# Layer 0 of a two-layer gated attention kernel: scores computed once, weights turned by VectorE and transfers

## The chip, the core and the metric

The kernel runs on one core of a Trainium2 chip. A core has a matrix engine (TensorE, PE in the profile, with its weight loads as PEld), three engines for elementwise work (VectorE or DVE, ScalarE or ACT, GpSimd or POOL), a SyncE (SP) that issues transfers, and 16 DMA engines that carry them out. Each engine works through its own queue in order and waits on semaphores for the others. Matrix products are written to PSUM, a small memory of 128 partitions and eight banks of 512 float32 each; everything else lies in SBUF, also with 128 partitions. The metric is the time of one execution in device microseconds.

## The reference, cut to what matters

Eight batches of 256 tokens of width 256 (`x`) and eight contexts of the same size (`ctx`) pass through two layers, each a gated cross attention followed by a gated feed-forward part. The change touches the first layer's attention:

```python
q, k, v = layernorm(x) @ Wq + bq, ctx @ Wk + bk, ctx @ Wv + bv      # 16 heads of 16
scores  = einsum('bhqd,bhkd->bhqk', q, k) / sqrt(16)
attn    = softmax(scores, axis=-1)                                   # 256 x 256 per head
out     = einsum('bhqk,bhkd->bhqd', attn, v).reshape(...) @ Wo + bo
x       = x + tanh(g_xattn[0]) * out
```

Behind it come a slot-routing feed-forward part per batch ("slots" below), a second attention with 8 heads of 128, where the 256 context rows are the queries' media and 512 keys stand against 256 queries, and a quantized feed-forward part that needs the maximum over all batches.

## The kernel before, in words

**Staging.** A first stretch prepares weights and works on batches 0 and 1 of layer 0 (attention and slots). Then `attention1` runs layer 1's attention, 8 batches x 8 heads, one head a step. Beside it a side queue holds the rest of layer 0, batches 2 to 7 with their slots, cut into pieces with costs. `side.share` works out how much of it is due so that batch b is ready before layer 1 comes to it, and each step spends half of that share after the head's softmax and half at its end. At the last batch the queue is drained, and the weights of the last feed-forward part are prepared. The tile framework schedules the instructions of each engine from this program order and from what it thinks the operations take, so pieces of both layers stand interleaved in every engine's queue. Tiles of a pool rotate through a fixed number of buffers, and a tile's next user waits for its last reader.

**Layer 0's attention for one batch** (`Batch0`). `query` and `key` project 256 tokens at once into one PSUM bank (L554), ACT adds the bias. Scores need more precision than one pass of the fast format float32r gives, so `split` (L520, L522) makes each operand the sum of a high part, rounded to float32r, and a low part; a product over 64 rows (hi hi lo lo against hi lo hi lo) restores it. For batches 0 and 1 `spread` builds these rows with selection matmuls. From batch 2 on, `split` writes the parts to DRAM and `stack` reads them back, with weights whose columns `by_place` has reordered so that a head's elements lie in the right places.

The 16 heads go in four groups of four. For each group the scores are computed twice:

- `scores`: queries on partitions. Eight matmuls of 65 rows (64 and one of blank) put four heads and two halves of the queries into PSUM (L648), VectorE finds each query's maximum (L651, four calls of 128x512), which is again split in two parts (L654, L655).
- `maxima`: one TensorE transposition (L661) and two ACT copies (L664) turn the maxima into rows 64 to 72 of the query operand.
- `exps`: eight matmuls of 73 rows with keys on partitions (L674), in which the maxima are subtracted by the extra rows. ACT takes the exponential of 128x512 at once (L677, four a group). The weights now stand with keys on partitions, as the next product needs them.
- `sums`: sixteen records of products with 32 columns each (L685) give the weighted values and, by a block of ones, the sums; `divide` turns them with a VectorE transposition (L708) and divides.

Layer 0's matmuls from batch 1 on use three PSUM banks, `bank_z`; layer 1 uses four, `bank_m`.

**Layer 1's attention** (`Batch1`) computes its scores once, with queries on partitions (L1170). The maximum (L1171) goes into the exponential as a bias (L1172). Then the weights are turned: VectorE transposes blocks of 32x32 (L1184) into a tile `z` with one buffer, and four transfers from SP (L1190) move the blocks to their partitions (`eT`). The keys are stored in a permuted order for that (`by_block`). `value` fills a tile for a pair of heads in two halves: the context half is copied out by ACT, the other by VectorE (L1147, L1154), both at the odd step before the pair. The query projection is L1087, the key L1124, the sums L1226, the output projection L1239.

The line that takes the scores twice, in `exps`:

```python
T.matmul(ps[:, kc, :], k[:, j, kc * P : (kc + 1) * P], q[:, j, :], start=True, stop=True)
```

Of the kernel before, what the change touches and what calls it, by code (L numbers as in the profile page):

```python
# [21 lines left out]
P = 128  # L22
# [3 lines left out]
HG = 4  # L26
# [23 lines left out]
IDLE_KEY = 10  # L50
IDLE_LATENTS = 8
# [55 lines left out]
def flamingo_kernel(ctx: ExitStack, tc: tile.TileContext, a: dict, out: bass.AP):  # L107
# [62 lines left out]
    wk_n, wq_n = xs[4], cs[4]  # L170
    wk, wq = (w0.tile([P, 2, D], F32, tag=n, name=n) for n in ("wk", "wq"))
    bk_n, bq_n = (pp_.tile([P, 2], F32, tag=n, name=n) for n in ("bkn", "bqn"))
    bk, bq = (w0.tile([P, 2], F32, tag=n, name=n) for n in ("bk", "bq"))
    nc.sync.dma_start(out=cs[0], in_=c_in[0])
    nc.sync.dma_start(out=wk_n, in_=a["L0_xattn_Wk"].rearrange("(c p) n -> p c n", p=P))
    nc.sync.dma_start(out=xs[0], in_=x_in[0])
    nc.sync.dma_start(out=wq_n, in_=a["L0_xattn_Wq"].rearrange("(c p) n -> p c n", p=P))
    for t, name in ((bk_n, "L0_xattn_bk"), (bq_n, "L0_xattn_bq")):
        nc.sync.dma_start(out=t, in_=a[name].rearrange("(c p) -> p c", p=P))
# [14 lines left out]
    def load_by_place():  # L194
        for m in range(2):
            for t, name in ((bk, "L0_xattn_bk"), (bq, "L0_xattn_bq")):
                bias = a[name].rearrange("(h e) -> e h", e=DK0)
                nc.sync.dma_start(out=t[:, m : m + 1], in_=bias[m * 8 : (m + 1) * 8, :])

    def by_place():  # L200
        for t, n in ((wk, wk_n), (wq, wq_n)):
            A.copy(t.rearrange("p c (e h) -> p c e h", e=DK0), n.rearrange("p c (h e) -> p c e h", e=DK0))
        G.tensor_scalar(bq4, bq, DK0**-0.5, None, ALU.mult)

# [4 lines left out]
    pick = w0.tile([NMAX, HG], F32, tag="pick", name="pick")  # L209
    V.tensor_tensor(pick, ident[:NMAX, 1 : 1 + HG], ident[:NMAX, 1 + HG : 1 + 2 * HG], ALU.add)  # L210

    def operand_pairs(pool, n):

        pairs = []
        for i in range(n):
            q = pool.tile([NROW + NMAX, HG, S], F32R, tag=f"qs{i}", name=f"qs{i}")
            k = pool.tile([NROW + NMAX, HG, S], F32R, tag=f"ks{i}", name=f"ks{i}")
            V.tensor_copy(q[NROW : NROW + 1, :, :], blank[:1, :HG, None].to_broadcast([1, HG, S]))
            V.tensor_copy(k[NROW:, :, :], pick[:, :, None].to_broadcast([NMAX, HG, S]))
            pairs.append((q, k))  # L220
        return pairs

    blank = w0.tile([P, 2 * HG], F32, tag="blank", name="blank")
    V.memset(blank, 0.0)

    pairs_a, pairs_b = operand_pairs(pp_, 2), operand_pairs(w0, 2)


# [102 lines left out]
    slotsT = pp_.tile([P, 2, P], F32, tag="slotsT", name="slotsT", bufs=1)  # L331
# [29 lines left out]
    def prepare_slots():  # L361
        st = {}

        def load_slots():
# [7 lines left out]
            st["w2"] = pp_.tile([NSLOT, P], F32, tag="w2n", name="w2n")  # L372
# [92 lines left out]
    bq4_n = pp_.tile([P, 2], F32, tag="bq4n", name="bq4n")  # L465
    G.tensor_scalar(bq4_n, bq_n, DK0**-0.5, None, ALU.mult)

    def values_tile(pool):
# [5 lines left out]
    halved = {  # L474
        s: [pool.tile([P, SIDE + NMAX], F32R, tag=f"nm{s}{i}", name=f"nm{s}{i}") for i in range(3)]
        for s, pool in (("a", pp_), ("b", w0))
    }
    for nm in halved["a"] + halved["b"]:
        V.tensor_copy(nm, blank[:, :1].to_broadcast([P, SIDE + NMAX]))
# [4 lines left out]
    class Batch0:  # L484
# [32 lines left out]
        def split(self, name, full):  # L517
# [7 lines left out]
            name += self.s  # L525
            d = dram.tile([2, D, S], F32, tag=f"d{name}", name=f"d{name}")
            for i, x in enumerate((hi, lo)):
                nc.sync.dma_start(out=d[i].rearrange("(m p) t -> p m t", p=P), in_=x.bitcast(F32))
            return d.rearrange("i (e h) t -> i e h t", e=DK0)
# [9 lines left out]
        def turn_c(self):  # L539
            self.cT = self.pool.tile([P, 2, S], F32, tag="cT", name="cT", bufs=1)  # L540
            A.copy(self.cT, self.turned(cs[self.b]))
# [21 lines left out]
        def query(self):  # L563
            w, bias = (wq_n, bq4_n) if self.b < 2 else (wq, bq4)
# [450 lines left out]
    for n, go in enumerate(first):  # L1015
# [3 lines left out]
        if n >= LAG:  # L1019
            second.pop(0)()  # L1020
# [738 lines left out]
```

## Time and profile before

| | |
|---|---|
| median of 3 runs | 915.75 us (913.85 to 917.1) |
| profiled execution | 917.64 us, span 915.7 us |
| PE busy | 877.0 us (96%) |
| PEld busy | 636.3 us |
| DVE busy | 639.8 us (70%) |
| ACT busy | 461.9 us (50%) |
| POOL busy | 143.1 us |
| bytes moved | 71.12 MB, hardware queue 29.0% of 16 DMA engines |
| granted TensorE clock | 0.992 |

The page gives, for every engine, the time in which at least one instruction ran. A busy PE is not a PE at its peak: matmuls overlap, so the distance from one start to the next is what one costs, and the mean of a group (382 ns for a record of L1226) is longer than that (0.216 us; a float32 matmul has two records). A table of stretches gives the same for parts of the span, named by their ends in microseconds. In the groups, the name before `<-` is the tile written, then come the tiles read, the shapes, the number of instructions, busy time and mean, and after the second bar the idle time of the engine just before them with what ended it. "eT<-z" in the lists of transfers is layer 1's turning of the weights, "qs<-dqb" and "ks<-dkb" are layer 0's stacks.

### The profile page before, as it was taken

How to read it: one execution, taken by the hardware profiler on the slowest of the kernel's cores; microseconds unless marked ns; L12 is line 12 of the kernel's file. 1: busy time of each engine (PE TensorE's matmuls, PEld its weight loads, DVE VectorE, ACT ScalarE, POOL GpSimd, SP SyncE). 2: the span in 40 equal slices, each digit the busy share in tenths (PEclk: the TensorE clock that was granted, in tenths of full speed). 3: DMA queues.
4: the chain of work that ended last, by engine and by line, in shares of the span. 5: the costliest groups of instructions: out<-in, count | busy, mean ns of one | idle time of the engine just before them, and what ended most of it. 6: DMA issues, size and time to landing. Idle time of an engine off the chain costs nothing. (4 is left out here: it accounts for less than half of the span.)

```text
span 915.7 us, 12787 instructions
## 1 busy us (share of the span) xinstructions
PE 877.0 (96%) x4339; PEld 636.3 (69%) x4341; DVE 639.8 (70%) x1630; ACT 461.9 (50%) x915; POOL 143.1 (16%) x183
## 2 busy tenths in 40 slices
PE   5998999999999999999999999999989999999897
PEld 4766777887777767766777667666756776776645
DVE  9675788777587766767677665766895475455387
ACT  3676646555356542555544544554364335434394
POOL 7011130201110112111011000010510010000083
PEclk9999999999999999999999999999999999999999
DMA  6712303342341332332312322212323232222112
GB/s 165 250 10 69 114 29 90 88 120 77 108 116 47 92 92 47 84 98 73 92 37 68 104 69 71 46 47 64 107 64 70 47 69 59 58 55 60 24 35 92
DMA packets 71728, 71.12 MB, mean 78 GB/s; under 512 B 14640, under 2 KB 67184, under 8 KB 71664
## 3 DMA queue, kind: packets, MB, share of 16 engines
q1 hardware_dynamic: 70032, 69.53, 29.0%
q0 software_dynamic: 1632, 0.79, 0.5%
q8 instruction: 35, 0.57, 0.3%
q14 instruction: 29, 0.24, 0.1%
HBM read 28.08 MB, written 8.39 MB: 40 GB/s over the span
## 5 line engine op out<-in xcount | busy, mean ns | idle before, releaser
L1172 ACT ACTIVATE e<-bank_m,nm 128x512 f32<-128x512 f32 x128 | 88.0, 688 | 107.5 <-DVE nm L1171 105.3
L1171 DVE TENSOR_REDUCE nm<-bank_m 128x1 f32<-128x512 f32 x128 | 87.1, 686 | 60.1 <-PE bank_m L1170 59.1
L1226 PE MATMUL bank_m<-eT,v 128*128 128x256 f32 x496 | 121.5, 382 | 4.6 <-DMA eT<-z 4.3
L1226 PEld LDWEIGHTS bank_m<-eT,v 128*128 128x128 f32 x496 | 92.4, 190 | 35.7 <-issue 16.6
L1124 PE MATMUL bank_m<-kvT,w1kv 128*128 128x512 f32 (+1 forms) x256 | 115.9, 568 | 0.0
L1147 PE MATMUL bank_m<-w1kv,kvT 128*128 128x256 f32 x480 | 111.0, 380 | 0.0
L1170 PE MATMUL bank_m<-k,q 128*128 128x512 f32 x224 | 108.9, 598 | 0.0
L1147 PEld LDWEIGHTS bank_m<-w1kv,kvT 128*128 128x128 f32 x480 | 89.4, 190 | 12.0 <-issue 0.8
L1184 DVE STREAM_TRANSPOSE z<-e 128x512 f32<-128x512 f32 x126 | 88.6, 706 | 4.3 <-DMA eT<-z 1.8
L651 DVE TENSOR_REDUCE nf<-bank_z 128x2 f32<-128x512 f32 x112 | 74.0, 680 | 20.7 <-PE bank_z L648 20.6
L270 POOL TENSOR_TENSOR rstd<-rstd,mhalf 128x2 f32<-128x2 f32 x48 | 34.6, 722 | 298.0 <-DVE rstd L269 267.7
L677 ACT ACTIVATE e<-bank_z 128x512 f32<-128x512 f32 x112 | 63.5, 598 | 32.7 <-PE bank_z L674 31.8
L1124 PEld LDWEIGHTS bank_m<-kvT,w1kv 128*128 128x128 f32 x256 | 46.4, 190 | 43.1 <-issue 38.0
L1233 ACT ACTIVATE oT<-bank_m,bv 128x256 f32<-128x256 f32 x64 | 30.4, 474 | 81.1 <-PE bank_m L1226 81.0
L1087 PE MATMUL bank_m<-kvT,w1q 128*128 128x256 f32 x256 | 64.0, 385 | 1.3 <-DVE kvT L1077 0.9
L1174 DVE TENSOR_SCALAR e<-e,rs 128x512 f32<-128x512 f32 x128 | 63.3, 495 | 2.6
L1239 PE MATMUL bank_m<-w1o,oT 128*128 128x256 f32 x256 | 59.2, 380 | 0.6 <-DVE x L1253 0.6
L1170 PEld LDWEIGHTS bank_m<-k,q 128*128 128x128 f32 x224 | 41.0, 191 | 23.4 <-issue 17.0
L1087 PEld LDWEIGHTS bank_m<-kvT,w1q 128*128 128x128 f32 x256 | 48.1, 192 | 12.4 <-issue 3.9
L1239 PEld LDWEIGHTS bank_m<-w1o,oT 128*128 128x128 f32 x256 | 48.0, 190 | 10.2 <-issue 3.2
L674 PE MATMUL bank_z<-qs,ks 73*128 73x256 f32 x224 | 49.8, 325 | 3.2 <-DVE nf L651 2.6
L1154 DVE COPY v<-bank_m 128x512 f32<-128x512 f32 x32 | 22.0, 688 | 44.0 <-PE bank_m L1147 44.0
(386 smaller groups left out, 1482.0 us busy)
## 6 DMA issues: line engine op xcount, KB each, us to landing
eT<-z SPq DMA_DIRECT2D x252, 128.0 KB, 2.7
qs<-dqb SPq DMA_DIRECT2D x96, 64.0 KB, 2.5
ks<-dkb SPq DMA_DIRECT2D x48, 128.0 KB, 2.8
c<-in_ctx_dram SPq DMA_DIRECT2D x8, 256.0 KB, 2.9
x<-in_x_dram SPq DMA_DIRECT2D x8, 256.0 KB, 2.8
w1kv<-in_L_xattn_Wkv_dram SPq DMA_DIRECT2D x4, 512.0 KB, 6.8
out_dram<-y SPq DMA_DIRECT2D x7, 256.0 KB, 2.2
dqb<-hi SPq DMA_DIRECT2D x6, 256.0 KB, 3.0
```

Source lines behind the costliest of these rows:

```text
L651: V.tensor_reduce(full[:, 2 * half : 2 * half + 2], ps, AX.X, ALU.max, negate=True)
L677: A.activation(e[:, i, :, :], ps, AF.Exp)
L1087: T.matmul(pq[:, i, :], w1q[:, c, h * P : (h + 1) * P], self.kvT[:, c, S:], start=c == 0, stop=c == 1,)
L1124: T.matmul(pk[:, at], w1kv[:, c, h * P : (h + 1) * P], self.kvT[:, c, at], start=c == 0, stop=c == 1,)
L1147: T.matmul(pv[:, k, :], (self.mT, self.kvT[:, :, S:])[half][:, c, k * P : (k + 1) * P], w1kv[:, c, at : at + 2 * P], start=c == 0, stop=c ...
L1170: T.matmul(ps, q, self.k[h], start=True, stop=True)
L1171: V.tensor_reduce(nm[:, at], ps, AX.X, ALU.max, negate=True)
L1172: A.activation(e[:, qc, :], ps, AF.Exp, bias=nm[:, at], accum_out=sums[:, at])
L1174: V.tensor_scalar(e[:, qc, :], e[:, qc, :], rs[:, at], None, ALU.mult)
L1184: V.transpose(z[:, :, :, qc, :].rearrange("p kq kc s -> p kc kq s"), self.e[h][:, qc, :].rearrange("p (kc kq k) -> p kc kq k", kc=4, kq=4),)
L1226: T.matmul(pi, self.v[h // 2][kc // 2][:, kc % 2, (h % 2) * P : (h % 2 + 1) * P], eT[:, kc], start=kc == 0, stop=kc == 3,)
L1239: self.projected = T.matmul(self.pp[:, qc, :], self.oT[:, h, qc * P : (qc + 1) * P], w1o[:, h, :], start=h == 0, stop=h == H1 - 1,).ins
```

## The change

From batch 1 on (the attention of batches 1 to 7; what goes through DRAM from batch 2 on), `weigh` replaces `scores`, `maxima` and `exps`. It takes half a group, two heads, in one call:

- A stack now holds two heads in 128 rows, head 0 in rows 0 to 63 and head 1 in 64 to 127 (tile 128x2x256 for a group). Four matmuls of 64 rows, two of each head, fill two banks.
- Per head VectorE finds the maxima (negated), and ACT takes two exponentials of 128x256 with the maxima as bias.
- VectorE transposes 32x32 blocks of 128x512 into `z0` (one buffer), and four transfers from SP bring the blocks to `eT0` (three buffers). `sums` reads `eT0`.
- Keys are stored in a permuted order by the ACT instruction that adds the bias, `turn_o` undoes the order of the queries in two calls.

Around it: the weights are no longer reordered (`by_place`, `load_by_place` and the second weight tiles go). `split` writes sixteen transfers a batch instead of four, `stack` reads two a group instead of six. The piece `weigh` has the cost 1.0, and its two calls for the next group stand before and after `sums` of the current one. Some tiles move into memory that is free early (`cT` of batch 0, the slots' turned states), the tiles of normalised tokens in layer 1 have one buffer instead of two, and layer 1's values have three half tiles instead of two whole ones, with the second half computed after the sums of the even head instead of at the odd step before.

```diff
+        def weigh(self, g, s):
+            q, k = self.pairs[g % 2]
+            ps = [self.bank().rearrange("p (c k) -> p c k", c=2) for _ in range(2)]
+            if s == 0:
+                self.idle(ps[0][:, 0, :], (IDLE_SCORES + ((0,) * NG,) * B)[self.b][g])
+            for qc in range(2):
+                for i in range(2):
+                    at = slice(i * NROW, (i + 1) * NROW)
+                    T.matmul(ps[i][:, qc, :], q[at, s, qc * P : (qc + 1) * P], k[at, s, :], start=True, stop=True)
+            z = at0.tile([P, 8, 2, 2, 32], F32, tag="z0", name="z0", bufs=1)
+            for i in range(2):
+                nm = small.tile([P, 2], F32, tag="nm0", name="nm0")
+                V.tensor_reduce(nm, ps[i], AX.X, ALU.max, negate=True)
+                e = at0.tile([P, 2, S], F32, tag="e", name="e", bufs=2)
+                for qc in range(2):
+                    A.activation(e[:, qc, :], ps[i][:, qc, :], AF.Exp, bias=nm[:, qc : qc + 1])
+                V.transpose(
+                    z[:, :, i, :, :].rearrange("p kb c s -> p c kb s"), e.rearrange("p c (kb k) -> p c kb k", k=32)
+                )
+            eT = self.e[g, s] = at0.tile([P, 4, 2, 2, 64], F32, tag="eT0", name="eT0", bufs=3)
+            for i in range(4):
+                nc.sync.dma_start(
+                    out=eT[:, i].rearrange("p kc h x -> p (kc h x)"),
+                    in_=z[32 * i : 32 * i + 32].rearrange("p kb h c s -> p (kb h c s)"),
+                )
...
@@ split
-            d = dram.tile([2, D, S], F32, tag=f"d{name}", name=f"d{name}")
-            for i, x in enumerate((hi, lo)):
-                nc.sync.dma_start(out=d[i].rearrange("(m p) t -> p m t", p=P), in_=x.bitcast(F32))
-            return d.rearrange("i (e h) t -> i e h t", e=DK0)
+            d = dram.tile([H0 * NROW, S], F32, tag=f"d{name}", name=f"d{name}")
+            for r, x in enumerate((hi, hi, lo, lo) if name == "q" else (hi, lo, hi, lo)):
+                to = d.rearrange("(m h r e) t -> r m h e t", m=2, r=4, e=DK0)[r]
+                for m in range(2):
+                    nc.sync.dma_start(out=to[m], in_=x[:, m, :].bitcast(F32))
+            return d.rearrange("(g s p) t -> g p s t", s=2, p=P)
...
@@ stack
+            for to, d in zip(self.pairs[g % 2], (self.dq, self.dk)):
+                ins = nc.sync.dma_start(out=to.bitcast(F32), in_=d[g])
...
@@ layer0
         def maxima(me, g):
+            if me.b > 0:
+                return [piece(COST_WEIGH, me, "weigh", g, s) for s in range(2)]
...
+                    work, ahead = ahead[:1], ahead[1:]
...
                 work.append(piece(1.8, me, "sums", g))
+                if b > 0:
+                    work += ahead
...
@@ Batch1.value, attention1
+                v = at1.tile([P, 2, 2 * P], F32, tag="v1", name="v1", bufs=3)
...
                 bs[last[0]].sums(last[1])
+            if h % 2 == 0 and n > 0:
+                me.value(h // 2, 1)
...
                     bs[nxt[0]].value(nxt[1] // 2, 0)
-                bs[nxt[0]].value(nxt[1] // 2, 1)
```

## The prediction

> **What bounds the kernel now.** I read the table of stretches first, then the chain of waits in order of time, then the groups by cost and the timeline of TensorE (PE) and SyncE (SP). The stretches were cut by the times of layer 1's score matmuls: its heads 4 to 16 run from 172 to 340 us, heads 16 to 40 from 340 to 641, the last 18 or so without any layer 0 beside them.
>
> ```profile
> core 0: us, PE busy (x) PEld busy (x) DVE busy (x) ACT busy (x) POOL busy (x), PEclk, DMA share, GB/s
> 172.00:340.00 168.00, 164.96 (x868) 123.09 (x867) 121.25 (x330) 86.93 (x176) 21.08 (x26) 0.99 0.34 92
> 340.00:641.00 301.00, 297.61 (x1441) 213.23 (x1440) 209.04 (x551) 145.44 (x293) 32.20 (x43) 1.00 0.27 70
> 700.00:850.00 150.00, 148.74 (x584) 104.56 (x582) 86.93 (x182) 64.64 (x143) 4.57 (x7) 1.00 0.26 59
> ```
>
> PE is busy 98 to 99% in all three, VectorE (DVE) 72, 69 and 58%. From 131 to 650 us layers 0 and 1 share one PE queue, and each microsecond of matmul taken out there should shorten the span, as long as nobody else becomes late.
>
> ```profile
> 143.76 0.83 PE L674 MATMUL bank_z<-qs,ks 73*128 73x256 f32 x4
> 144.42 0.40 PE L648 MATMUL bank_z<-ks,qs 65*128 65x256 f32 x2
> 144.66 0.60 PE L1167 MATMUL bank_m<-c,q 128*128 128x256 f32 x2
> ```
>
> The second scores (L674) hold PE from 143.76 to 144.42, 0.165 us each with the change of kind; two of L648 take 0.24, so 0.12 each. The groups give the rest:
>
> ```profile
> L674 PE MATMUL bank_z<-qs,ks 73*128 73x256 f32 x224 | 49.8, 325 | 3.2 <-DVE nf L651 2.6
> L651 DVE TENSOR_REDUCE nf<-bank_z 128x2 f32<-128x512 f32 x112 | 74.0, 680 | 20.7 <-PE bank_z L648 20.6
> L1184 DVE STREAM_TRANSPOSE z<-e 128x512 f32<-128x512 f32 x126 | 88.6, 706 | 4.3 <-DMA eT<-z 1.8
> L677 ACT ACTIVATE e<-bank_z 128x512 f32<-128x512 f32 x112 | 63.5, 598 | 32.7 <-PE bank_z L674 31.8
> L664 ACT CAST qs<-bank_z 9x512 fp32r<-9x512 f32 x56 | 32.2, 575 | 16.1 <-PE bank_z L661 15.4
> L1233 ACT ACTIVATE oT<-bank_m,bv 128x256 f32<-128x256 f32 x64 | 30.4, 474 | 81.1 <-PE bank_m L1226 81.0
> L654 DVE CAST nmb<-nf 128x4 fp32r<-128x4 f32 x56 | 9.5, 170 | 0.4
> L655 DVE TENSOR_TENSOR nmb<-nf,nmb 128x4 fp32r<-128x4 f32 x56 | 8.8, 156 | 0.5
> eT<-z SPq DMA_DIRECT2D x252, 128.0 KB, 2.7
> 319.65 2.50 SPq L1190 DMA_DIRECT2D eT<-z  x4
> ```
>
> L1184 and the eT transfers are layer 1's own turning of weights, which the change copies into layer 0: 0.706 us of DVE per 128x512, four issues of 2.50 us on SP, 2.7 us to land.
>
> **The change part by part.** A group is four heads of one batch; the new code reaches batches 1 to 7, 28 groups, of which batch 1's four lie before 131 us.
>
> PE. Per group, eight L674 and the transposition of maxima (L661) go; the eight first scores stay. Eight at 0.12 to 0.165 are 0.96 to 1.32 us; L661 takes 0.20 (300.91 to the next start at 301.11). I take 8 x 0.145 + 0.20 = 1.36 us, 38 us in all, 32.6 of it in the shared stretch and 5.4 before.
>
> The first scores change form, from 65 rows to 64 at two row offsets into two banks. If pairs run side by side, they cost half: 56 calls x 0.29 = 16 us less. If they don't, and each call adds a break like that around the 32-column products L685 (16 records in 1.00 us, where 16 x 0.216 / 4 is 0.86), 56 x 0.14 = 8 us more. I take nothing, halfway between unknown ends.
>
> The Trainium skill, "TensorEngine Tiling (Array Packing)", Key Properties, says that changing the tiling mode drains TensorE, which speaks against 64-row calls among full ones; the L685 row shows such a break at 0.14 us at most. The same page promises up to twice the speed at 64 rows or fewer; by the one the sum is 8 us worse, by the other 16 better, and no row here shows which.
>
> DVE. Per group four transpositions of 0.706 come, two L654 and two L655 go: 2.82 - 0.65 = 2.17 us, 61 us over 28 groups. The four maxima keep their size. Turning the output in two halves costs 2 x 0.44 (L708's size) for one of 0.709, 0.2 per batch. Counted in the changed instruction order, 38 maxima fall between heads 4 and 16 and 42 between 16 and 36, 9.5 and 10.5 groups. So in the first stretch DVE has 121 + 21 = 142 us and PE 168 - 13 = 155: 92%. In the second 209 + 23 = 232 against 301 - 14 = 287: 81%. That is the price that has to be found.
>
> How PE fares beside a full DVE the profile shows itself. Of the slices of 25 us from 125 to 675, five have DVE over 20 us: PE is idle there 0.82, 0, 0.28, 0.67 and 0.91 us, on average 0.54, at most 0.91. Over the 440 us that remain that is 9.5 us, at most 16; at least 0, as in the second of them.
>
> ScalarE (ACT). Eight exponentials of 128x256 at 0.474 (L1233's size) replace four of 0.598 and two casts of 0.575: 3.79 for 3.54, 7 us in all on an engine half idle. Nothing; if the cover is gone, 7.
>
> SP and DMA. Per group eight issues of about 0.63 and two stacks replace six (0.79 + 1.81 by the timeline): 5.8 for 2.6 us. Per batch 16 split issues replace four; at 0.38 (L528) to 0.80 (a 32 KB L192 issue) 6 to 13 us for 1.5. Over six batches that is 104 to 146 us more on SP, whose queue then stands at some 60% of the shared stretch instead of a third. 28 MB of weights and 6 MB of split writes join 69.5 MB at 29.0%: 43%. Both stay under their limits, but a 2.5 us burst can now stand ahead of layer 1's own eT, and on SP every transfer waits for its own source with all later ones behind it.
>
> The wait that is new: the weighted sums (L685, now fed by transfers) wait for the landing. From the end of the scores: two maxima 1.4, or one and four exponentials 2.6, one transposition 0.7, three issues 1.9, and 2.7 for the fourth to land: some 7.9 us with every engine free. Layer 1's same chain has a landing of 2.6 to 4.2 alone between 340 and 641 us, so 9 is likelier there. In the changed PE order I summed the matmuls that stand between a group's last scores and its sums: from 7.0 us up, six of 28 under 9. Their shortfalls add to 6.5 us at a latency of 9, to 29 at 11 and to nothing at 7. I take 6.5. Behind the waiting sums on PE stand layer 1's scores, for which DVE and ACT wait.
>
> Moved: layer 1's second half of a value pair (L1147, 1.73 us of PE, one DVE copy of 0.69) goes behind the sums of the next even head, past that head's maxima on DVE and its four eT issues on SP, past nothing on POOL. Its reader is a head later, 8.6 us on PE: nothing; if late, 0.7 per pair. One buffer instead of two for the normalised tokens: its three users stand at separate heads, so nothing; 0.6 (four transpositions) per use if not.
>
> Start. Two sets of setup casts (2 x 0.96 + 2 x 0.81), two 1.05 us ACT copies of weights and four bias loads go. The first key projection starts at 10.90, right after the second context's transpositions at 10.42 that waited for its transfer; the changed order puts two more transpositions and five warm-up matmuls ahead of it, 0 to 1 us later. Of batch 1's 5.4 us I count half, because before 131 us PE is not full (21.8 to 22.9 of 25).
>
> Sum: 32.6 + 2.7 - 9.5 - 6.5 = 19 us off the profiled execution's 917.64 us (span 915.7 and 1.9 around it), that is 898.6. The profiled execution stands 1.9 above the median of 915.75, so I forecast 897.
>
> **Rivals.**
> A, slower: DVE takes the lead through the single z buffer. A second call's transpositions wait until the first's four transfers have read z; DVE works in order, so layer 1's maxima stand behind them and PE runs dry. For: 16 of the calls in the changed PE order follow the one before by under 3 us, while z is held until about 7.9 us after the scores. Against: layer 1's z is single too, and L1184 waits only 1.8 us for it. It decides from 35.3 / 48 = 0.74 us of PE idle per call in the shared stretch, instead of the 0.33 of my sum; at 1.0 it gives 917.6 - 35 + 48, less 1.9: about 929.
> B, faster still: pairs of 64-row scores run side by side and waits stay at the low end: 19 + 16 = 35 less, some of it stopped by DVE's 92%: 878 to 888.
> C, nothing: the sums' latency is 11 us rather than 9. 19 - 22 = -3; with part of it hidden, 912 to 918.
>
> **How the numbers follow.** Mine 0.50, B 0.22, C 0.12, A 0.16. A measurement of this kernel tells about 0.3% (2.7 us) from no change: under 913 is faster, over 918.5 slower. Mine and B are all faster, C splits 0.04, 0.06, 0.02. Faster 0.76, same 0.06, slower 0.18. My own case's range is 887 to 908, from stalls of 7 to 27 us. To leave out two in ten I reach down into B to 877 and up through C to 917; A lies outside.
>
> **What would show it.** Right: no second scores, PE still over 97% in the shared stretch and layer 0's last sums some 30 us earlier; DVE total near 640 + 58 = 698, over 85% busy in the first half of the shared stretch; sums' waits on eT a few us in total. Wrong: PE under 95% with long waits for DVE's maxima or z (A), sums' waits over 20 us (C), or four scores in well under 0.5 us (B).

## The result, and the profile after

The changed kernel takes 944.04 us (median of four runs, 942.1 to 950.09) against 915.06 for the kernel before: a ratio of 1.0326, with a 95% interval of 1.0275 to 1.0376. The forecast was 897, so the step that was to take 19 us away added 29.

The table of stretches of the changed kernel, cut at the same heads of layer 1 (4 to 16, 16 to 40, and the last part without layer 0); the columns are those of the table before:

```profile
core 0: us, PE busy (x) PEld busy (x) DVE busy (x) ACT busy (x) POOL busy (x), PEclk, DMA share, GB/s
186.20:371.90 185.70, 164.72 (x778) 112.97 (x777) 143.97 (x361) 85.26 (x196) 24.98 (x32) 0.94 0.59 157
371.90:670.40 298.50, 289.04 (x1310) 198.01 (x1309) 222.40 (x536) 137.72 (x305) 34.52 (x44) 0.99 0.43 109
735.00:885.00 150.00, 148.73 (x584) 105.62 (x583) 83.32 (x174) 63.31 (x140) 4.57 (x7) 1.00 0.26 59
```

Heads 16 to 40 take 298.5 us instead of 301, and in the last part TensorE is as busy as before. The first row is where time goes: it takes 185.7 us instead of 168, with TensorE busy for the same 165 us: 89% instead of 98. VectorE is at 78% there, not at the 92% forecast, because the stretch is longer. The DMA share went from 0.34 to 0.59, and the granted clock from 0.99 to 0.94. The rest of the loss lies ahead of this table: layer 1's first head starts at 146.8 us instead of 131.2.

The page's totals, the hardware queue's share, and three groups of VectorE:

```profile
PE 868.5 (92%) x4089; PEld 606.0 (64%) x4089; DVE 683.9 (73%) x1631; ACT 447.6 (48%) x961; POOL 141.1 (15%) x182
...
q1 hardware_dynamic: 115952, 105.19, 43.0%
```

```profile
L674 DVE STREAM_TRANSPOSE z<-e 128x512 f32<-128x512 f32 x112 | 75.0, 692 | 30.2 <-DMA eT<-z 26.7
...
L1200 DVE STREAM_TRANSPOSE z<-e 128x512 f32<-128x512 f32 x126 | 87.7, 702 | 3.9 <-DMA eT<-z 2.0
L670 DVE TENSOR_REDUCE nm<-bank_z 128x2 f32<-128x512 f32 x112 | 72.9, 677 | 21.0 <-PE bank_z L666 20.7
```

Of the forecast's quantities the DMA share (43.0%, forecast 43) and a transposition's 692 ns (forecast 706) came out as said. VectorE's total came near (684, forecast 698), though its rise was 44 us and not 58. TensorE's did not: its busy time fell by 8.5 us (877.0 to 868.5) instead of 38, and its idle time, summed over the gaps between matmuls, rose from 30.3 to 64.7. Layer 0's last sums, forecast some 30 us earlier, start 17 us later (604.1 us instead of 587.2).

TensorE's waits in the changed kernel (total, times, longest). Before, its waits for layer 1's eT came to 4.3 (the line shown second), and there were none for a stack (ks, qs, now kt, qt):

```profile
engine line waited for: us in total, times, longest us
PE bank_z L666 <- DMA kt<-dk: 9.4, 4, 3.7
PE bank_m L1242 <- DMA eT<-z: 8.8, 4, 3.6
PE bank_z L693 <- DMA eT<-z: 7.6, 8, 2.0
...
PE bank_z L743 <- DVE oT L736: 4.7, 2, 4.2
```

```profile
PE bank_m L1226 <- DMA eT<-z: 4.3, 3, 2.0
```

**Where TensorE's time went.** Counting each matmul record from its start to the next start (less idle time) gives what a line costs. By that count the second scores (L674 of before) fell by 37.4 us and the transposed maxima (L661) by 5.6: 43.0, where the forecast had 38. The first scores went from 38.1 to 32.7 in batches 1 to 7, the sums of all batches from 33.0 to 35.9. Against that saving of some 46 us, all the other lines together, whose work is unchanged, cost 38 us more, and idle time is 34 us more.

**The clock.** A part of the 38 us is the clock. The clock's record begins 16.3 us into the span of the kernel before and 14.4 us into that of the changed one; the earlier time is left out here, and so is the very end. It has four stretches at half clock in the kernel before, 3.41 us each. In the changed one there are thirteen such units, so nine more: 31 us at half clock, up to 15 us of work lost. They stand behind TensorE's gaps. The stretches around one of them, 3.4 us with a wait for kt, the 6.8 after it, and the next 3.4:

```profile
256.80:260.20 3.40, 0.13 (x1) 0.00 (x0) 0.69 (x1) 0.93 (x3) 0.00 (x0) 1.00 0.85 237
260.20:267.00 6.80, 6.33 (x25) 2.72 (x26) 4.86 (x10) 2.35 (x6) 0.00 (x0) 0.50 0.43 140
267.00:270.40 3.40, 3.40 (x13) 2.05 (x12) 2.70 (x8) 0.79 (x2) 0.00 (x0) 1.00 0.31 93
```

The last column but two is the granted clock: 1.00 while TensorE stood idle, 0.50 for the two units after. In both traces every unit of 3.41 us with 1.8 us or more of idle TensorE is followed by half clock. Those with 1.5 to 1.7 at full clock are not, and some that have 0.7 to 1.4 are. In all nineteen traces of this case, from the start of the clock's record to 12 us before the end, each of the 90 units at full clock with 2.0 us or more of idle is followed by half clock, and 29 of the 90 with 1.5 to 2.0; so the 1.8 of these two traces is no sharp limit. A wait of 2 us within one unit therefore cost 2 here and then up to another 1.7 or 3.4. The Trainium skill ("TensorE: Matmul & The Clock Gate", Part 1) says that the clock halves after an idle window of about 3.4 us; the window's length agrees, but here 2.0 us of idle in a window was enough.

**One of the waits for kt, followed back.** SyncE's queue and TensorE's in the changed kernel (start, duration, line, what is moved):

```profile
start us, us, engine line op out<-in xcount [idle before <-releaser]
324.65 2.48 SPq L679 DMA_DIRECT2D eT<-z  x4
327.24 1.31 SPq L506 DMA_DIRECT2D dk<-hi  x2
328.66 1.19 SPq L506 DMA_DIRECT2D dk<-lo  x2
329.89 1.18 SPq L506 DMA_DIRECT2D dk<-hi  x2
331.12 1.18 SPq L506 DMA_DIRECT2D dk<-lo  x2
332.41 0.57 SPq L604 DMA_DIRECT2D qt<-dq  x1
335.65 0.88 SPq L604 DMA_DIRECT2D kt<-dk  x2
```

```profile
334.39 1.02 PE L1186 MATMUL bank_m<-k,q 128*128 128x512 f32 x2
335.25 0.38 PE L912 MATMUL bank_s<-ident,hn 128*128 128x128 f32 x2
338.47 0.63 PE L666 MATMUL bank_z<-kt,qt 64*128 64x256 f32 x4 [2.84 <-DMA kt<-dk]
```

The next batch's key is split; SP issues its eight writes (L506) from 327.24 to 332.30. The read of kt (L604) needs them landed and goes out at 335.65, and the first scores (L666) start at 338.47, after 2.84 us of nothing on TensorE. Half clock follows from 338.7. Of the four waits for kt in this trace, two are followed at once by half clock, this one and the longest (3.74 us, at 260.67); the other two, 1.25 and 1.57 us, are not. Before, a split had two writes per operand instead of eight.

### The profile page after: what moved, and what is told of

It is laid out like the page before. It is cut to its first block, busy times and chain, and to the rows that moved or that the text cites. A ratio compares the mean times of both kernels' runs of the same rounds, so it can differ in the third digit from the quotient of the medians.

```text
span 941.9 us, 12794 instructions
## 1 busy us (share of the span) xinstructions
PE 868.5 (92%) x4089; PEld 606.0 (64%) x4089; DVE 683.9 (73%) x1631; ACT 447.6 (48%) x961; POOL 141.1 (15%) x182
## 5 line engine op out<-in xcount | busy, mean ns | idle before, releaser
L673 ACT ACTIVATE e<-bank_z,nm 128x256 f32<-128x256 f32 x224 | 90.0, 476 | 67.7 <-DVE nm L670 56.0
L1163 PE MATMUL bank_m<-w1kv,kvT 128*128 128x256 f32 x480 | 115.1, 382 | 0.1
L1186 PE MATMUL bank_m<-k,q 128*128 128x512 f32 x224 | 110.7, 609 | 0.6 <-DVE v L1170 0.6
L674 DVE STREAM_TRANSPOSE z<-e 128x512 f32<-128x512 f32 x112 | 75.0, 692 | 30.2 <-DMA eT<-z 26.7
L1200 DVE STREAM_TRANSPOSE z<-e 128x512 f32<-128x512 f32 x126 | 87.7, 702 | 3.9 <-DMA eT<-z 2.0
L670 DVE TENSOR_REDUCE nm<-bank_z 128x2 f32<-128x512 f32 x112 | 72.9, 677 | 21.0 <-PE bank_z L666 20.7
L1190 DVE TENSOR_SCALAR e<-e,rs 128x512 f32<-128x512 f32 x128 | 65.7, 514 | 2.1
L1112 ACT ACTIVATE q<-bank_m,bq 128x256 f32<-128x256 f32 x64 | 26.8, 471 | 82.1 <-PE bank_m L1103 82.0
L1186 PEld LDWEIGHTS bank_m<-k,q 128*128 128x128 f32 x224 | 41.3, 192 | 30.2 <-issue 19.6
L1170 DVE COPY v<-bank_m 128x512 f32<-128x512 f32 x32 | 21.8, 682 | 46.2 <-PE bank_m L1163 46.2
```

The costliest lines, as they stand in the source:

```text
L670: V.tensor_reduce(nm, ps[i], AX.X, ALU.max, negate=True)
L673: A.activation(e[:, qc, :], ps[i][:, qc, :], AF.Exp, bias=nm[:, qc : qc + 1])
L674: V.transpose(z[:, :, i, :, :].rearrange("p kb c s -> p c kb s"), e.rearrange("p c (kb k) -> p c kb k", k=32))
L1163: T.matmul(pv[:, k, :], (self.mT, self.kvT[:, :, S:])[half][:, c, k * P : (k + 1) * P], w1kv[:, c, at : at + 2 * P], start=c == 0, stop=c ...
L1186: T.matmul(ps, q, self.k[h], start=True, stop=True)
L1200: V.transpose(z[:, :, :, qc, :].rearrange("p kq kc s -> p kc kq s"), self.e[h][:, qc, :].rearrange("p (kc kq k) -> p kc kq k", kc=4, kq=4),)
```

## The experiments

Each kernel was timed beside the kernel before on the same chip, and ratios are to those runs. Differences between kernels are worked out as differences of ratios times 915 us.

### Taking the turning away, in two steps

The first kernel leaves the turning out, and the exponentials go straight to the tile that the sums read:

```diff
-            z = at0.tile([P, 8, 2, 2, 32], F32, tag="z0", name="z0", bufs=1)
+            eT = self.e[g, s] = at0.tile([P, 4, 2, 2, 64], F32, tag="eT0", name="eT0", bufs=3)
+            flat = eT.rearrange("p i c h x -> p (i c h x)").rearrange("p (i c k) -> p i c k", i=2, c=2)
...
-                    A.activation(e[:, qc, :], ps[i][:, qc, :], AF.Exp, bias=nm[:, qc : qc + 1])
-                V.transpose(
...
+                    A.activation(flat[:, i, qc, :], ps[i][:, qc, :], AF.Exp, bias=nm[:, qc : qc + 1])
-            for i in range(4):
-                nc.sync.dma_start(
...
```

The second leaves out only the transfers; z is a view of that tile, and the transpositions stay:

```diff
-            z = at0.tile([P, 8, 2, 2, 32], F32, tag="z0", name="z0", bufs=1)
+            eT = self.e[g, s] = at0.tile([P, 4, 2, 2, 64], F32, tag="eT0", name="eT0", bufs=3)
+            z = eT.rearrange("p i c h x -> p (i c h x)").rearrange("p (b h c s) -> p b h c s", b=8, h=2, c=2)
...
-            for i in range(4):
-                nc.sync.dma_start(
...
```

> Leaves out layer 0's turning of the weights from batch 1 on: ScalarE writes the exponentials straight into the tile that the sums read (so the sums multiply unturned weights), no VectorE transposition, no transfer. Everything else is as after the change. Counted from start to next start, TensorE's own work of the group fell by 46 us (second scores 37.4, maxima 5.6, scores 38.1 to 32.7, sums 33.0 to 35.9, small 0.8). Theory T (the loss is the turning's transfers: SP's queue and the wait for their landing) and theory D (the loss is VectorE's load) both expect 865 to 882 us, with TensorE idle near the 30 us of before and four or five stretches at half clock. Theory P (the loss is in TensorE's new form of work or in the other added transfers, the 64-row calls and the split's 16 writes a batch) expects 900 or more.

> Leaves out only the four transfers behind each of layer 0's calls: VectorE transposes straight into the tile that the sums read (so its blocks stand on the wrong partitions). VectorE's work is that of the changed kernel (684 us busy). T expects 870 to 890 us, within 10 us of the kernel without any turning; D expects 915 to 940, TensorE waiting for VectorE as often as after the change.

Without turning: 913.5 us, ratio 0.9982 (0.9959 to 1.0005). Without transfers: 916.28, ratio 1.0015 (0.999 to 1.004). So VectorE's 112 transpositions cost some 3 us in the end, hardly more than the intervals allow for nothing, and their transfers 28. That difference is what speaks against theory D, VectorE's load: 916 us alone would lie in D's range, and T's forecasts for both kernels failed too. The first kernel lies in theory P's range, 900 or more. Even with no turning at all the change gains nothing, so 46 us of saved TensorE work are lost elsewhere. TensorE's waits without turning:

```profile
PE bank_z L666 <- issue: 7.6, 2, 4.4
PE bank_z L666 <- DMA kt<-dk: 5.8, 3, 3.0
...
PE bank_m L1233 <- DMA eT<-z: 3.7, 3, 1.7
```

The first scores L666 now wait most, 15.2 us of idle time in front of them, most of it in five long gaps at 177.5, 201.2, 235.7, 319.0 and 403.8 us, most of them a batch apart. The profile puts 5.8 us down to kt; for the 7.6 under "issue" it shows no cause.

### The key's chain

`key` is moved from the third group of a batch to the second, in the kernel without turning, in the changed kernel, and in the kernel before as a control:

```diff
...
                         work.append(piece(1.8, after, "query"))
+                        work.append(piece(1.8, after, "key"))
-                    if g == 2:
-                        work.append(piece(1.8, after, "key"))
```

> Leaves out layer 0's turning from batch 1 on, as in the first run of this study (913.5 us), and places the key projection one group earlier. There TensorE waited 15.2 us in front of the first scores L666, in five places about a batch apart, and six windows of 3.4 us at half clock followed such waits (10 us lost). K expects 886 to 900 us. If it is the 64-row calls or the clock by itself that eat the 46 us of saved work: 908 to 916.

> Whole computation; the next batch's key projection, with its split and eight writes, is placed in the group of the query (g == 1) instead of one group later, some 20 us earlier. Theory K: the chain key, split, eight writes from SP, landing, kt's read, landing is late at each batch's first scores (9.4 us of waits for kt in four places after the change, each followed by 3.4 to 6.8 us at half clock): 924 to 934 us. If the earlier writes only push the weights' transfers back on SP: 938 to 948.

> The kernel before, with the key projection one group earlier, and nothing else: a control of the 13 us that this place gave without the turning. Before the change TensorE never waited for a stack (no kt or ks among its waits), so theory K expects no change, 912 to 918 us. If the place by itself is worth something, 900 to 908.

Without turning it gives 900.47 us, ratio 0.9843 (0.9803 to 0.9883), 13 us better. The first scores' idle time falls from 15.2 to 4.6 us; the half-clock units within the span fall from ten to seven. Its waits:

```profile
PE bank_m L1232 <- DMA eT<-z: 4.9, 5, 1.7
...
PE bank_z L666 <- DMA kt<-dk: 2.3, 2, 1.4
```

The control got slower, 920.47 (1.0057, 1.0036 to 1.0079), so the place as such isn't worth anything. That the chain is late because the change made it longer fits both runs. In the whole changed kernel the move gave nothing (942.87, 1.0302): the waits for kt left the list, but the sums' waits for their own weights rose from 7.6 to 11.9 us and the waits for layer 1's normalised latents from 1.5 to 7.1.

The splits' 16 writes a batch from GpSimd's queue instead of SP's:

```diff
-                    nc.sync.dma_start(out=to[m], in_=x[:, m, :].bitcast(F32))
+                    nc.gpsimd.dma_start(out=to[m], in_=x[:, m, :].bitcast(F32))
```

> Whole computation; the split's 16 writes a batch are issued by GpSimd's queue instead of SP's. T, in the form that SP's order is what is late: the waits of the first scores for kt (9.4 us in four waits, each followed by 3.4 to 6.8 us at half clock) go, and part of the sums' waits: 924 to 934 us. If SP's order doesn't matter, or GpSimd's issues are as late as SP's: 940 to 948. D expects 940 to 946.

943.02 us, 1.0313: nothing gained. The waits for kt are still 8.3 us and layer 1's for its eT 12.1. The writes landed in 3.6 to 4.7 us from GpSimd.

### The form of the scores

The kernel without turning and with the early key, its scores in 65 rows at one offset. The stacks are laid out for it, so the reads of qt and kt fill 64 partitions with four heads instead of 128 with two:

```diff
-                    at = slice(i * NROW, (i + 1) * NROW)
-                    T.matmul(ps[i][:, qc, :], q[at, s, qc * P : (qc + 1) * P], k[at, s, :], start=True, stop=True)
+                    at, j = slice(NROW + 1), 2 * s + i
+                    T.matmul(ps[i][:, qc, :], q[at, j, qc * P : (qc + 1) * P], k[at, j, :], start=True, stop=True)
```

> Leaves out layer 0's turning and places the key one group earlier, as the run before that gave 900.5 us, and takes the new scores with 65 rows at one row offset (64 and one of zeros, the form of the kernel before) instead of 64 rows at two offsets. In the changed kernel a block of L666 costs 93 ns on the record before it and 105 ns on the one behind, 72 such blocks; its pairs start 3 ns apart and then hold TensorE for 220, where two records of 65 rows take 2 x 119. Theory F (the form costs a break each time and gives nothing back): 12 us less, 886 to 892. If the form is free: 897 to 904.

What the 64-row calls do shows in TensorE's timeline of the changed kernel:

```profile
419.90 1.07 PE L693 MATMUL bank_z<-eT,ve 128*32 128x256 f32 x16
420.91 0.50 PE L666 MATMUL bank_z<-kt,qt 64*128 64x256 f32 x4
421.34 1.99 PE L1186 MATMUL bank_m<-k,q 128*128 128x512 f32 x4
423.16 1.88 PE L1140 MATMUL bank_m<-kvT,w1kv 128*128 128x512 f32 x4
```

The call's four records take 0.43 us to the next line's start (420.91 to 421.34), where four of 65 rows took 4 x 0.119. In the trace the two records of a pair start 3 ns apart and then hold TensorE for 220 and 207 ns: 0.11 us a record, so being side by side makes a pair hardly shorter than two in a row. The four L1186 behind take 1.82 us instead of 4 x 0.429: the record ahead of such a block takes 93 ns longer, and the one behind it 105. There are 72 blocks, which makes 14 us of the 38 in the other lines.

897.17 us, ratio 0.9806 (0.9779 to 0.9832). TensorE's busy time with 64 rows and with 65:

```profile
PE 854.9 (95%) x4089; PEld 599.1 (67%) x4089; DVE 627.1 (70%) x1519; ACT 446.5 (50%) x961; POOL 141.4 (16%) x182
```

```profile
PE 843.9 (94%) x4089; PEld 606.9 (68%) x4089; DVE 626.4 (70%) x1523; ACT 450.9 (50%) x969; POOL 142.5 (16%) x182
```

That is 11.0 us, as the breaks and pairs add up to (12). But the span fell by 3 to 5 only, and by the ratios, whose intervals overlap, no gain is settled. The first scores' waits for kt came back, and the run can't tell whether the other layout of the reads brought them:

```profile
PE bank_z L666 <- DMA kt<-dk: 6.9, 4, 3.1
```

### The transfers: which part of them

Layer 0's transfers from another queue, all from GpSimd in one kernel, half of them from ScalarE in the other:

```diff
-                nc.sync.dma_start(
+                nc.gpsimd.dma_start(
```

```diff
-                nc.sync.dma_start(
+                (nc.sync if i < 2 else nc.scalar).dma_start(
```

> Whole computation; layer 0's 224 transfers of weights are issued by GpSimd's queue instead of SP's. T in the form that SP's order is late expects 915 to 932 us, if GpSimd issues one in about SP's 0.63 us; in the form that the landing itself is late (whichever queue issues it) 940 to 950. D expects 940 to 946. If GpSimd takes over 1 us for one, or its norm work stands in front, 950 or more.

> Whole computation; of the four transfers behind each of layer 0's calls two are issued by ScalarE's queue instead of SP's. SP's burst halves to 1.25 us and its queue loses some 70 us. If SP's order is late: 922 to 935 us. If ScalarE, half idle but in order, stands waiting for z with layer 1's exponentials behind it: 945 to 965.

985.23 us (1.0771) and 957.9 (1.0463): both slower than SP alone. GpSimd issued four in 2.17 us, no slower than SP. But with its other work in the same queue the waits for kt rose to 15.0 us and the sums' own to 12.0. In the second kernel VectorE's waits for z stayed at 26.6 us and kt's rose to 15.9.

A second z for the second call of each group, in batches 2 to 4. It lies over a tile that also holds layer 1's first values, so those are overwritten:

```diff
+            if s == 1 and 2 <= self.b <= 4:
+                z = last.rearrange("p i t d -> p (i t d)").rearrange("p (b h c s) -> p b h c s", b=8, h=2, c=2)
+            else:
+                z = at0.tile([P, 8, 2, 2, 32], F32, tag="z0", name="z0", bufs=1)
-            z = at0.tile([P, 8, 2, 2, 32], F32, tag="z0", name="z0", bufs=1)
```

> Whole computation; the second call of each group of batches 2 to 4 turns its weights in a second z tile, laid in the place of batch 7's tokens, which are loaded later. VectorE stood idle 26.7 us for z in 22 places, most before 400 us. Theory Z (rival A of the prediction: the single z holds VectorE, and layer 1's work behind it) expects 926 to 936 us. If the hold is cover (SP's issues are what is late, so the second transposition only waits elsewhere): 940 to 947.

942.21 us, ratio 1.0288 (1.0251 to 1.0325): nothing that can be told from the changed kernel. VectorE's wait for z, in the changed kernel and here:

```profile
DVE z L674 <- DMA eT<-z: 26.7, 22, 3.1
```

```profile
DVE z L680 <- DMA eT<-z: 16.2, 12, 3.4
```

Ten us less of waiting for z, and no time gained.

Then the turning was done in full, but into a tile that nothing reads:

```diff
+                e = flat[:, i]
...
+            dump = at0.tile([P, 4, 2, 2, 64], F32, tag="dump", name="dump", bufs=1)
             for i in range(4):
                 nc.sync.dma_start(
-                    out=eT[:, i].rearrange("p kc h x -> p (kc h x)"),
+                    out=dump[:, i].rearrange("p kc h x -> p (kc h x)"),
                     in_=z[32 * i : 32 * i + 32].rearrange("p kb h c s -> p (kb h c s)"),
```

Then with a quarter of the bytes in as many issues, and with all the bytes in one transfer:

```diff
-                    out=dump[:, i].rearrange("p kc h x -> p (kc h x)"),
-                    in_=z[32 * i : 32 * i + 32].rearrange("p kb h c s -> p (kb h c s)"),
+                    out=dump[:, i, 0, 0, :],
+                    in_=z[32 * i : 32 * i + 32, 0:2].rearrange("p kb h c s -> p (kb h c s)"),
```

```diff
-            for i in range(4):
...
+            nc.sync.dma_start(
+                out=dump.rearrange("p i kc h x -> p (i kc h x)"), in_=z.rearrange("p kb h c s -> p (kb h c s)")
+            )
```

A fourth kernel is the one without transfers, with the four transfers to "dump" behind each call: they copy from the tiles of the sums, so VectorE waits for no single z. In a fifth, "dump" of the second call lies in the place of batch 7's tokens.

> Turns the weights in full (transpositions, z, four transfers from SP), but into a tile that nothing reads; the sums read the exponentials unturned, so their products are of the wrong weights. Against the changed kernel (944) only the sums' wait for the landing is gone; against the one without transfers (916.3) SP's issues, z's hold and the DMA load are there. Theory L (the 28 us of the transfers are the sums' own wait for the landing): 916 to 925. Theory Q (SP's queue and the transfers make others late: layer 1's own weights, kt, VectorE behind z): 934 to 944.

> As the run whose turned weights nothing reads (938.4 us), but each of the four transfers of a call moves a quarter of the bytes (128 rows of 256 bytes for 1 KB); SP issues as many. Theory S (SP's time for issues, with everything behind them in its order, is what the transfers cost): 934 to 940. Theory B (the bytes: full DMA engines land layer 1's weights and kt later and hold z longer): 916 to 926.

> As the same run (938.4 us), but a call's turned weights go in one transfer of the same bytes (128 rows of 4 KB, not moved across partitions) instead of four: SP issues 56 instead of 224. S expects 916 to 926; B expects 932 to 940.

> As the run without transfers (916.3 us; VectorE transposes straight into the three tiles that the sums read), and behind each call four transfers of full size copy that tile into one that nothing reads. SP's issues and the bytes are those of the changed kernel; what is gone against the run with unread weights (938.4) is that VectorE waits for a single z. Theory B (bytes and DMA engines): 932 to 940. Theory Z (z's hold of VectorE, rival A): 915 to 924.

> As the same run (938.4 us), but in batches 2 to 4 the second call of a group writes into another unread tile (in the place of batch 7's tokens, over some of layer 1's first values, so batch 0's output differs in that too): there SP stood waiting 37.9 us in 39 places for the last transfer into the one unread tile, a wait that the changed kernel doesn't have. If that wait carries the run's loss: 920 to 930. If not, 934 to 940, and the run's verdict stands.

Unread: 938.36 us, ratio 1.024 (1.021 to 1.027). A quarter of the bytes: 920.53, 1.0055 (1.0034 to 1.0076). One transfer: 925.54, 1.0115 (1.0094 to 1.0135). No hold by z: 934.16, 1.018 (1.0134 to 1.0226). Two unread tiles: 944.63, but there layer 1's sums waited 9.1 us once for a transfer into the borrowed place, a wait that the edit itself brought, so this run doesn't settle what it was made for: whether SP's wait for the last transfer into the one unread tile, which the changed kernel doesn't have, carries the loss of these runs. The other traces speak against it. That wait came to 37.9 us in the unread kernel, 21.8 with a quarter of the bytes, 57.3 with one transfer and 46.0 with no hold, and the kernel that waited longest, with one transfer, is the second fastest of the four.

The hardware queue's share in the pages of the runs without transfers, with a quarter of the bytes, with one transfer, and with no hold, in this order:

```profile
q1 hardware_dynamic: 83696, 75.81, 30.7%
```

```profile
q1 hardware_dynamic: 115952, 83.17, 34.7%
```

```profile
q1 hardware_dynamic: 91760, 105.18, 38.4%
```

```profile
q1 hardware_dynamic: 115952, 105.19, 43.3%
```

In these four the time goes with this share: 30.7% and 916.3 us, 34.7 and 920.5, 38.4 and 925.5, 43.3 and 934.2. The share alone doesn't set the time, though: the unread kernel has 43.3% and takes 938.4, the changed kernel 43.0% and 944.0. The quarter of the bytes has the same number of packets and of issues on SP as full size, and gave back 17 us of the 21 that unread transfers cost. That is as theory B, the bytes, forecast, and S, SP's time for issues, falls as the main cause. One transfer kept the bytes and still gave back 11, against B's forecast. Its rows of 4 KB took less of the DMA engines' time and it has a quarter of the issues, and the run can't tell these apart. The sums' own wait for the landing is 8 us (1.0326 to 1.024), VectorE's wait for a single z some 5 (1.024 to 1.018; the ends overlap, so that isn't settled).

### The whole computation with fewer bytes

Exponentials, turned weights and values of layer 0 in float16 from batch 1 on; and the same with the freed room used, both calls of the next group ahead of the sums, and the key early as above:

```diff
-            z = at0.tile([P, 8, 2, 2, 32], F32, tag="z0", name="z0", bufs=1)
+            z = at0.tile([P, 8, 2, 2, 32], F16, tag="z0", name="z0", bufs=1)
-            eT = self.e[g, s] = at0.tile([P, 4, 2, 2, 64], F32, tag="eT0", name="eT0", bufs=3)
+            eT = self.e[g, s] = at0.tile([P, 4, 2, 2, 64], F16, tag="eT0", name="eT0", bufs=3)
```

```diff
-            z = at0.tile([P, 8, 2, 2, 32], F16, tag="z0", name="z0", bufs=1)
+            z = at0.tile([P, 8, 2, 2, 32], F16, tag="z0", name="z0", bufs=2)
-            eT = self.e[g, s] = at0.tile([P, 4, 2, 2, 64], F16, tag="eT0", name="eT0", bufs=3)
+            eT = self.e[g, s] = at0.tile([P, 4, 2, 2, 64], F16, tag="eT0", name="eT0", bufs=5)
...
-                    work, ahead = ahead[:1], ahead[1:]
+                    work, ahead = ahead, []
```

> Whole computation with layer 0's exponentials, turned weights and values from batch 1 on in float16 instead of float32: the transfers move half the bytes in as many issues, and the sums take one pass instead of two. From the runs with unread weights, full bytes 938.4 and a quarter 920.5, half the bytes are worth some 12 us; half of the sums' 36 us of records at 28 groups of 32 would be at most 14 more. B expects 914 to 932. If SP's issues carry the loss, 932 to 944.

> The same in float16, and with the room that this frees: two z tiles, five tiles of turned weights, both calls of the next group ahead of the sums of this one (the sums have a call's time more, and the 64-row calls stand in half as many blocks), and the key projection one group earlier. If waits behind transfers and breaks are what eats the saved work: 890 to 908, below the kernel before. If something else holds: 912 to 930.

927.67 us, 1.0112 (1.0063 to 1.0162), as B expected: 20 us better than the changed kernel. Fewer bytes (37.2% of the hardware queue) and the sums in one pass share in it and aren't told apart; TensorE's busy time fell by 14 us (868.5 to 854.2). The second: 924.04 us, 1.008 (1.0059 to 1.0101), still slower than the kernel before and short of its forecast. Its waits:

```profile
PE bank_z L666 <- DMA kt<-dk: 8.8, 3, 3.6
PE bank_m L1241 <- DMA eT<-z: 8.4, 6, 4.1
PE bank_z L666 <- ACT e L673: 8.1, 6, 3.2
```

The sums no longer wait (0.7 us). Layer 1's own eT, kt, and now ScalarE's exponentials do. With two calls in a row the second probably waits for banks that the first's exponentials hold.

## Why the prediction was wrong

**The step that failed** is "SP and DMA", with its "Both stay under their limits" and its price of nothing. The load was sized right (43.0% of the DMA engines, forecast 43), the price was not: the paragraph names the danger, a burst ahead of layer 1's eT and transfers behind one another on SP, and puts no term for it into the sum. Without layer 0's transfers the kernel takes 28 us less; of that the forecast had 6.5, the sums' wait. Between the profiled executions with and without these transfers (941.9 and 918.3 us) TensorE's idle time differs by 15.4 us and its busy time by 8.1. Its waits named as the sums' own, for kt and for layer 1's eT make 25.8 us with the transfers (7.6, 9.4 and 8.8) and 12.6 without (none, 5.6 and 7.0). Why the load of the engines turns into these waits is argued and not shown: shares of 0.34 to 0.59 in a stretch are means over bursts, and what should count is when a transfer that TensorE needs next stands behind others. The traces with this many transfers give no landing times for most single ones.

**Key's split**, 13 us in the kernel without turning and nothing measurable in the changed one, where other waits took its place. The forecast counted its 16 issues as a load on SP and didn't follow the chain of which they are the first link: key, eight writes, landing, kt, landing, first scores. In the profile before nothing waited for this chain, so it doesn't show there. A chain of transfers should have been laid against the time to its reader, as was done for the sums.

**The clock** was in no term of the sum. Nine more units at half clock, up to 15 us, come on top of the waits, and make a wait of 2 us nearly twice as dear.

**The form of the scores.** Forecast 0, bounds -16 and +8 us: TensorE's busy time says +11, beyond the upper end, and the span +3, not settled. The break is 0.20 us for a block (0.093 and 0.105) instead of 0.14, and there are 72 blocks instead of 56, because other lines' matmuls stand between a call's own. The Trainium skill's rule that spoke against the change ("TensorEngine Tiling (Array Packing)", Key Properties: a change of tiling mode drains TensorE) agrees with these numbers; its speed-up at 64 rows does not show, since a pair takes 0.22 us where two single records take 0.24.

**The start**, forecast 2.7 us better, came out 15.6 worse. Without transfers layer 1's first head starts at 142.0 us, without any turning at 130.1. These times can't be read as costs one by one, because the order of the instructions moves with the kernel: TensorE has done 110.2 us of work by then without any turning, 118.5 without transfers, 116.8 in the changed kernel and 113.0 before. Of the 15.6 us some 4 are such work, and nearly 12 are idle time of TensorE (30.0 us against 18.2). Batch 1's share stands in a stretch where TensorE's gaps were taken from its busy share (21.8 to 22.9 of 25) and not from what it waits for: chains.

**Right**: TensorE's removed work (43.0 against 38), the transposition's length, the bytes, the sums' wait (8 against 6.5), the cover over ScalarE's exponentials. Too dear: the stall by VectorE's share, 9.5 against some 3. Too high: the busy time added on VectorE (44 us, forecast 58 to 61) and on ScalarE, whose total fell by 14 (461.9 to 447.6) where 7 more were forecast. The forecast added up durations, and busy time counts what overlaps once: the 224 exponentials of 128x256 last 0.476 us each, 107 in all, and keep ScalarE busy for 90.0.

**The rivals.** A gave 929 and was nearest, but not for its reason: VectorE's wait for z is there (26.7 us), a second z for batches 2 to 4 changed nothing, and taking the hold away whole is worth some 5 us, not settled. TensorE's idle time in the shared stretch is 31.3 us. Over A's 48 calls that is 0.65 each, over the 43 that start there in the changed kernel 0.73, and A's turning point, from which nothing is gained, was 0.74. Idle time of that size alone would have left the time as it was; what made it slower is TensorE's busy time, which fell by 8.5 us instead of 38 (clock and breaks), and the idle time ahead of that stretch. B's pairs start side by side in the trace and gain next to nothing. C's 22 us of the sums' latency would be 8.

**What stays open.** Without turning, with the early key and 65 rows the kernel takes 897.17 us, 18 less than before, where 46 us of records were saved and 33 show in TensorE's busy time. Idle time is 43.1 us against 30.3, and 13 us of the saving don't show in TensorE's busy time; this wasn't taken apart further. In the changed kernel itself, of the 38 us that the lines with unchanged work cost more, the clock (up to 15) and the breaks (14) leave some 9 open. And no kernel here that computes the whole beats the one before.

## What to carry to other kernels

When an operation on the bounding engine is replaced by transfers, don't take a share of the DMA engines under its limit for free: 28 us stood behind 43% here. For each transfer that the engine will read, lay issue, landing and everything ahead of it against the time until the reader, also for operands that only change their layout. Look at the clock's record beside the waits: a wait of 2 us on TensorE could cost nearly 4 in this kernel. And a saving on the bounding engine is worth only as much as the rest can follow: here 46 us of removed matmuls were worth 18 at best.

## What the runs showed that was not expected

- 2.0 us of idle TensorE in a unit of 3.41 us were enough for half clock in the next (90 of 90 such units in all traces), in the changed kernel in four of nine stretches for the next two (6.8 us).
- Two 64-row float32r matmuls of 256 columns at two row offsets start 3 ns apart and hold TensorE 0.22 us, hardly less than two of 65 rows in a row (0.24).
- 29 MB of transfers that nothing reads cost 21 us against none, SP's wait for the one unread tile included; a quarter of the bytes in as many issues and packets cost 4.
- A float16 transposition of 128x512 on VectorE took 690 ns on average, as long as one in float32 (692).
